# Offset bound on ScalarE, a third tap on TensorE, one product for the roots, and key rows stored in two parts

## The chip, the cores and the metric

The program runs on one core of one Trainium2 chip. A core has five instruction streams that run side by side and meet only through semaphores: TensorE (PE in the profile, with its weight loads as PEld), VectorE (DVE), ScalarE (ACT), GpSimd (POOL) and SyncE (SP), which here only starts DMA transfers. Sixteen DMA engines carry out the transfers. The metric is the device time of one execution in microseconds, from the first instruction to the last; lower is better.

## The reference, cut to what matters

The network has four layers over x of shape 8 x 56 x 56 x 128 in float32. Two of them are touched.

Layer 0 is a deformable convolution with a small MLP behind it. For each image:

```python
xp = x @ w_in + b_in
h = gelu(batch_norm(depthwise_conv_3x3(x) + dw_b))
offset = (h @ w_off + b_off)                       # 4 groups x 9 points x (x, y)
mask = softmax((h @ w_msk + b_msk), over the 9 points)
y = bilinear_samples(xp, at 3x3 grid + offset, weighted by mask) @ w_out + b_out
x = x + gamma1 * layer_norm(y)
x = x + gamma2 * layer_norm(gelu(x @ w_fc1 + b_fc1) @ w_fc2 + b_fc2)
```

Layer 1 whitens x. Layer 2 is self-attention with 8 heads of 16 channels, where queries, keys and values are one projection (`h = x @ W_k.T`), and then a mixture of experts. Layer 3 is linear attention and another mixture of experts. Of layers 1 and 3 and of the experts nothing is changed.

## The kernel before, in words

Within one layer's scope the instructions are put in order by a planner: the program text gives the data dependences and the priority (earlier text first), and the planner, which has its own idea of how long things take, lets a later instruction go ahead on an engine when an earlier one isn't ready. Buffers are rings of `bufs` tiles; a ring's next tile waits until the one that it replaces is released by all its readers. Attention itself (`attend`) is ordered by hand. A run-time `If` stands at the end of each of three stages, and nothing moves across it.

**Stage A, `conv_layer`, lines 128 to 398: the first half of layer 0.** The constants are loaded, and a tile of zeros (L236) is stored by ScalarE's DMA queue into the two edge rows at the top and bottom of `strips` (L239 to L242) and into the edge columns (L243 to L247). Then the images go through a software pipeline (L377 to L389). `image` loads one image, transposes it (L266), copies it into a padded picture (L271) and stores a copy `xT` (L276 to L279). `first_taps` makes the first `NTE` = 2 of the nine depthwise taps on TensorE, as products with a diagonal matrix per tap (L315), seven blocks of 448 columns, and ScalarE copies each block to `acc` (L322). `other_taps` adds the other seven on VectorE, one instruction for each tap over the whole picture of 128 x 3136 (L327). `projection` makes `xp` for two images at a time (L288, L295) and stores it (L301 to L305). `hidden` is the gelu on ScalarE (L341). `offsets` makes offsets and mask scores (L356, L363), takes the largest offset and the largest negative offset over 112 x 2016 numbers with two VectorE reductions (L365, L366) into two columns of `far`, does the softmax (L430 to L435, its exponential on ScalarE at L432) and stores the result (L370). At the end the maximum of `far` over all (L393 to L397) is compared with 1.0 (L398): only if no offset is beyond one pixel is the fast way of sampling taken, and the inputs at hand do take it.

**Stage B, `sample_near`, `norm` and `mlp`, lines 447 to 655.** Sampling is done as products with 88-row windows; the weights of the next image are built (L490 to L513) and transposed (L523, L525) while the current image is in flight. Each image has 7 groups of 448 columns, and each group passes through `norm` twice, 112 times in all. `norm` (L593 to L622) works on channels by pixels: squares on ScalarE (L600), sums of squares as products with a column of 1/128 (L604), which come out as `rs`, 112 pixels x 4, then + eps (L608) and the power -0.5 on GpSimd (L609). The roots have to be spread over the 128 channels for the product at L621. That is done by four products (L614): the weights are a column of `rs` repeated 128 times, the moving side is the 112 x 112 identity.

**Stage C** is layer 1.

**Stage D, `attention_keys`, lines 1039 to 1133.** For each of the 8 images: two loads (L1062), a store of the same tokens (L1063), layer norm (L1067, L1068, L1141, L112), transposes (L121, L122), then the keys `kT`: for each of two groups of four heads a tile of 128 rows, head j in rows 32j to 32j+15, a row of ones in 32j+16, and zeros in 32j+17 to 32j+31 (they come out of padded weights and a bias, L1083 to L1092). The tile has one buffer (`bufs=1`). Each group is stored whole to `kT_d` by SP, 128 rows of 12,544 bytes (L1094). Then the values (L1098 to L1108) are stored (L1110), and a bound is taken (L1117 to L1120). All transfers of this stage are on SP's queue. Behind the stage comes an `If`, and then `attend` loads keys and values part by part (L1222, L1224).

**Stage E** is `attend`, and **stage F** the rest.

Of the kernel before, what the change touches and what calls it, by code (L numbers as in the profile page):

```python
# [17 lines left out]
NB, IH, IW, C = 8, 56, 56, 128  # L18
S = IH * IW
T = 112  # L20
# [15 lines left out]
R4 = 4 * C  # L36

NPX = 6
NTE = 2


WB, WCOLS, WSTEP, WITER, WEPS = 64, NB * S * C // 64, 9, 5, 0.01
# [20 lines left out]
def make_consts(tc, pool):  # L63
    nc = tc.nc
    k = Consts()
    k.ident = pool.tile([128, 128], F32, name="ident")
    make_identity(nc, k.ident)
    k.eps = pool.tile([128, 1], F32, name="eps_col")
    nc.vector.memset(k.eps, EPS)
    k.mhalf = pool.tile([128, 32], F32, name="mhalf")  # L70
    nc.vector.memset(k.mhalf, -0.5)
    k.part = pool.tile([128, 1], F32, name="part_of_c")
    nc.vector.memset(k.part, 1.0 / C)
    k.ones = pool.tile([1, 128], F32, name="ones_row")
# [50 lines left out]

def conv_layer(tc, k, x, w, z):

    nc = tc.nc  # L130
    n_batch = x.shape[0]
    with ExitStack() as ctx:
# [63 lines left out]
        gam = row_bc(nc, cp, w["gamma2"], T, "gam2r")  # L196
        nc.vector.tensor_tensor(q.sft2, q.sft2, gam, ALU.mult)

        far = cp.tile([T, 2 * n_batch], F32, name="far")
        near = cp.tile([1, 1], I32, name="near")  # L200
        with ExitStack() as pre:
            ip = pre.enter_context(tc.tile_pool(name="l0i", bufs=1))
# [11 lines left out]
                "b_om",  # L214
            )
            b_om = b_om.unsqueeze(1).to_broadcast([T, GT, 3 * GP])

            dw = ip.tile([C, 9], F32, name="dw")
            nc.sync.dma_start(dw, w["dw_w"].rearrange("c a b d -> c (a b d)"))
# [13 lines left out]
            nc.vector.tensor_tensor(bn_t, bn_t, bn_s, ALU.mult)  # L233
            nc.vector.tensor_tensor(bn_t, bn_t, bn_b, ALU.add)

            zero = ip.tile([NX * n_batch, 2 * SW * C], F32, name="zero")  # L236
            nc.gpsimd.memset(zero, 0.0)
            rows = q.strips.rearrange("n k y s c -> (n k) y (s c)")
            for y in (0, VW - 2):  # L239
                nc.scalar.dma_start(  # L240
                    rows[:, y : y + 2].rearrange("k y s -> k (y s)"), zero
                )  # L242
            for n in range(n_batch):  # L243
                for at in (q.strips[n, 0, :, :2], q.strips[n, NX - 1, :, SW - 2 :]):
                    nc.scalar.dma_start(
# [104 lines left out]
            def offsets(n, hT):  # L350

                om = hp.tile([T, NT, 3 * GP], F32, name="om")
                for r in range(PH):
                    p = ps.tile([T, GT, 3 * GP], F32, tag="m", name="p_om")
                    for i in range(GT):
                        nc.tensor.matmul(  # L356
                            p[:, i, :],
                            hT[:, r, i].rearrange("p a b -> p (a b)"),
                            w_om,
                            start=True,  # L360
                            stop=True,
                        )
                    nc.vector.tensor_tensor(om[:, r * GT : (r + 1) * GT, :], p, b_om, ALU.add)  # L363
                off = om[:, :, : 2 * GP]
                nc.vector.tensor_reduce(far[:, 2 * n : 2 * n + 1], off, AX.XY, ALU.max)  # L365
                nc.vector.tensor_reduce(  # L366
                    far[:, 2 * n + 1 : 2 * n + 2], off, AX.XY, ALU.min, negate=True
                )
                mask_softmax(nc, hp, om)
                nc.sync.dma_start(q.om[n], om)  # L370


# [4 lines left out]
            for n in range(-1, n_batch + 1):  # L377
# [10 lines left out]
                if n > 0:  # L388
                    offsets(n - 1, hT)  # L389


            top = ip.tile([T, 1], F32, name="far_top")
            nc.vector.tensor_reduce(top, far, AX.X, ALU.max)  # L393
# [1 line left out]
            nc.tensor.transpose(p, top, k.ident[:T, :T])  # L395
            one = ip.tile([1, 1], F32, name="far_one")
            nc.vector.tensor_reduce(one, p, AX.X, ALU.max)  # L397
            nc.vector.tensor_scalar(near, one, 1.0, None, ALU.is_le)  # L398

        taken = nc.values_load(near[0:1, 0:1], min_val=0, max_val=1)  # L400
        with tc.If(taken > 0) as both:
# [191 lines left out]
def norm(tc, k, wp, ps, p, bias):  # L593


    nc = tc.nc
    y = wp.tile([C, QC], F32, name="y")
    nc.scalar.activation(y, p[:, :QC], AF.Identity, bias=bias)
    sq = wp.tile([C, QC], F32, name="sq")
    nc.scalar.activation(sq, p[:, :QC], AF.Square, bias=bias)  # L600
    yield
    var = p[:T, QC : QC + GT]
    for i in range(GT):
        nc.tensor.matmul(  # L604
            var[:, i : i + 1], sq[:, i * T : (i + 1) * T], k.part, start=True, stop=True
        )
    rs = wp.tile([T, GT], F32, name="rs")
    nc.vector.tensor_scalar(rs, var, EPS, None, ALU.add)  # L608
    nc.gpsimd.tensor_tensor(rs, rs, k.mhalf[:T, :GT], ALU.pow)  # L609
    yield  # L610

    p = ps.tile([C, QC], F32, tag="m", name="p_rs")
    for i in range(GT):
        nc.tensor.matmul(  # L614
            p[:, i * T : (i + 1) * T],
            rs[:, i : i + 1].to_broadcast([T, C]),
            k.ident[:T, :T],
            start=True,
            stop=True,
        )  # L620
    nc.vector.tensor_tensor(y, y, p, ALU.mult)  # L621
    return y  # L622

# [415 lines left out]
def attention_keys(tc, k, w, yv, tok, kT_out, va_out, low, small):  # L1039
# [6 lines left out]
    with ExitStack() as ctx:  # L1046
# [12 lines left out]
        for n in range(n_b):  # L1059
            t_sb = bp.tile([T, NT, C], F32, name="t")  # L1060
            for h in range(2):
                nc.sync.dma_start(t_sb[h * IW : (h + 1) * IW], yv[h, n])  # L1062
            nc.sync.dma_start(tok[n].rearrange("(t p) c -> p t c", p=T), t_sb)  # L1063
            mv = bp.tile([T, NT, 2], F32, name="mv")
            st = bp.tile([T, NT, 6], F32, name="st")
            for i in range(NT):
                nc.vector.bn_stats(st[:, i], t_sb[:, i])  # L1067
                nc.vector.bn_aggr(mv[:, i], st[:, i])  # L1068
            rs = rsqrt(nc, k, bp, mv, NT)
            xT = bp.tile([C, S], F32, name="xT")  # L1070
            for g in range(NG):
                xn = bp.tile([T, GT, C], F32, name="xn")
                for i in range(GT):
                    normalize(nc, xn[:, i], t_sb[:, g * GT + i], mv, rs, g * GT + i)
                transpose_group(
                    nc, k, ps, "m", xT[:, g * QC : (g + 1) * QC], xn, nc.scalar.copy
                )
            kT = bp.tile([128, 2, S], F32, name="kT", bufs=1)
            for g in range(2):
                for c in range(NG):  # L1080
                    cols = slice(c * QC, (c + 1) * QC)
                    p = ps.tile([128, QC], F32, tag="m", name="p_h")
                    nc.tensor.matmul(  # L1083
                        p, wk[:, g * 128 : (g + 1) * 128], xT[:, cols], start=True, stop=True
                    )
                    if c % 2:
                        nc.scalar.activation(
                            kT[:, g, cols], p, AF.Identity, bias=w.one16, scale=DK**-0.25
                        )
                    else:  # L1090
                        nc.vector.tensor_scalar(
                            kT[:, g, cols], p, DK**-0.25, w.one16, ALU.mult, ALU.add  # L1092
                        )
                nc.sync.dma_start(kT_out[n, g], kT[:, g])  # L1094
            va = vas[n % 2]
            for t, m in key_tiles():
                p = ps.tile([128, 2, 4, DK], F32, tag="m", name="p_v")
                nc.tensor.matmul(  # L1098
                    p[:m].rearrange("p g j d -> p (g j d)"),
                    xT[:, t * 128 : t * 128 + m],  # L1100
                    w.wv,
                    start=True,
                    stop=True,
                )
                if t % 2:
                    nc.scalar.copy(va[:m, :, t, :, :DK], p[:m])
                else:
                    nc.vector.tensor_copy(va[:m, :, t, :, :DK], p[:m])  # L1108
            for g in range(2):
                nc.sync.dma_start(va_out[n, g], va[:, g].rearrange("p t j d -> p (t j d)"))  # L1110

            sq = bp.tile([128, 2 * KT * 4, DK], F32, name="sq", bufs=1)
            v = va.rearrange("p g t j d -> p (g t j) d")[:, :, :DK]
            nc.gpsimd.tensor_tensor(sq, v, v, ALU.mult)  # L1117
            top = bp.tile([128, 2 * KT * 4], F32, name="top")
            nc.vector.tensor_reduce(top, sq, AX.X, ALU.add)
            nc.vector.tensor_reduce(tops[:, n : n + 1], top, AX.X, ALU.max)  # L1120
# [1056 lines left out]
    return t, b  # L2177


def token_layers(tc, k, a, y, out):  # L2180

    nc = tc.nc
    n_b = out.shape[0]
    with ExitStack() as ctx:
# [3 lines left out]
        t_c = [dp.tile([S, C], F32, name=f"t_c{n}") for n in range(n_b)]  # L2188
        t_g = dp.tile([n_b, S, C], F32, name="t_g")
        tok = [dp.tile([S, C], F32, name=f"tok{n}") for n in range(n_b)]  # L2190
        kT_d = dp.tile([n_b, 2, 128, S], F32, name="kT_d")
# [99 lines left out]
def conv_attn_hybrid_kernel(ctx, tc, a, out):  # L2291
# [7 lines left out]
    conv_layer(tc, k, a["x"], w, z)  # L2299
    whiten_layer(tc, k, z, y)  # L2300
    token_layers(tc, k, a, y, out.rearrange("n h w c -> n (h w) c"))


# [40 lines left out]
```

## Time and profile before

| what | value |
|---|---|
| time, median of 3 runs | 7714.85 us (7708.21 to 7727.53) |
| the profiled execution's own time | 7718.14 us |
| its span, first to last instruction | 7716.3 us |
| PE busy | 6482.3 us, 84% of the span |
| DVE busy | 5284.8 us, 68% |
| ACT busy | 4142.6 us, 54% |
| POOL busy | 2935.1 us, 38% |
| DMA queue of SP (q1) | 1260.76 MB, 65.1% of 16 engines' time |
| HBM read and written | 286.04 MB and 197.81 MB |

The stages stand one behind the other, so a mean over the span tells little; a table of busy time by stage is the first thing to look at. Lines of the profile name the source line (L327), the engine, the operation, the tiles, the shapes and the count, then the busy time, the mean of one in ns, and the idle time before them with what ended it. In the view by stretches, each engine's busy us and count are followed by the granted TensorE clock (1.00 is full), the mean busy share of the 16 DMA engines and the GB/s that they moved. The profile's packet records give start, length and size of each piece that a DMA engine moved; they say when, but not on which of the sixteen.

### The profile page before, as it was taken

To read this page: it belongs to the slowest core of one execution; us is meant where nothing else is said; L and a number is where in the kernel's file an instruction comes from. 1 tells how busy PE (TensorE), PEld (TensorE's weight loads), DVE (VectorE), ACT (ScalarE), POOL (GpSimd) and SP (SyncE) were. 2 spreads that over 40 slices of the span, in tenths; PEclk is the share of its full clock that TensorE was granted. 3 is DMA by queue.
4 is the path that set the end of the run, shared out by engine and by line. 5 is a ranking of instruction groups with operands and counts; after the bars stand their busy time and mean duration, and the time that the engine had idled before them with its cause. 6 is when DMAs were issued, how large, how long until landed. Compare 5 with 4: busy or idle time off the path is not lost. (4 is left out here: it accounts for less than half of the span.)

```text
span 7716.3 us, 157926 instructions
## 1 busy us (share of the span) xinstructions
PE 6482.3 (84%) x59883; PEld 2880.7 (37%) x59883; DVE 5284.8 (68%) x9856; ACT 4142.6 (54%) x6467; POOL 2935.1 (38%) x2555
## 2 busy tenths in 40 slices
PE   6659999556899999999999999999999997556654
PEld 4446666334233323323323323333333333245532
DVE  7975564366677777777777777777777776366752
ACT  4424444122666666666666666666666664056740
POOL 0011111022444444444444444444444443434653
PEclk8768898777999999999999999999999998788766
DMA  5453443376788778778778778778778775543543
GB/s 155 137 119 76 86 95 65 82 240 207 199 203 197 193 192 199 189 192 201 191 184 204 188 183 207 183 191 205 185 190 206 182 190 137 196 117 107 134 135 130
DMA packets 736303, 1287.38 MB, mean 167 GB/s; under 512 B 117698, under 2 KB 503108, under 8 KB 728516
## 3 DMA queue, kind: packets, MB, share of 16 engines
q1 hardware_dynamic: 725556, 1260.76, 65.1%
q0 software_dynamic: 6144, 12.60, 0.6%
q8 instruction: 484, 7.93, 0.5%
q10 hardware_dynamic: 3824, 3.68, 0.2%
q14 instruction: 295, 2.42, 0.1%
HBM read 286.04 MB, written 197.81 MB: 63 GB/s over the span
## 5 line engine op out<-in xcount | busy, mean ns | idle before, releaser
L1260 ACT ACTIVATE e<-p_s 128x768 f32<-128x768 f32 (+2 forms) x3712 | 2887.8, 830 | 1584.9 <-PE p_s L1252 1329.8
L1298 POOL COPY x<-sq 32x1152 f32<-32x1152 f32 x1792 | 2059.2, 1149 | 2067.6 <-PE p_s L1252 1330.0
L1271 DVE STREAM_TRANSPOSE sq<-e 128x768 f32<-128x768 f32 x2688 | 2434.5, 950 | 567.3 <-ACT e L1260 312.9
L1252 PE MATMUL p_s<-q,kT 32*128 32x384 f32 (+2 forms) x14848 | 1888.6, 548 | 33.6 <-ACT e L1260 18.6
L1305 PE MATMUL av<-e,va 128*32 128x384 f32 (+2 forms) x14848 | 1645.3, 515 | 30.4 <-DVE acc L1324 20.7
L1305 PE MATMUL avx<-x,va 128*32 128x384 f32 x10752 | 1138.3, 496 | 69.5 <-issue 40.2
L1252 PEld LDWEIGHTS p_s<-q,kT 32*128 32x128 f32 (+1 forms) x14848 | 654.8, 181 | 1252.6 <-issue 825.4
L1305 PEld LDWEIGHTS av<-e,va 128*32 128x32 f32 (+1 forms) x14848 | 294.5, 108 | 1049.4 <-issue 941.7
L1305 PEld LDWEIGHTS avx<-x,va 128*32 128x32 f32 x10752 | 353.2, 111 | 650.9 <-issue 595.2
L609 POOL TENSOR_TENSOR rs<-rs,mhalf 112x4 f32<-112x4 f32 x112 | 116.1, 1036 | 788.3 <-DVE rs L608 788.3
L1324 DVE TENSOR_TENSOR acc<-acc,avx 128x384 f32<-128x384 f32 x336 | 183.9, 547 | 229.9 <-PE avx L1305 228.6
L121 PE MATMUL p_tr<-ident,xn 112*128 112x112 f32 x672 | 134.6, 341 | 187.4 <-DVE xn L112 141.8
L1141 POOL TENSOR_TENSOR rs<-rs,mhalf 112x4 f32<-112x4 f32 (+2 forms) x136 | 168.1, 1236 | 269.3 <-DVE ntop L1942 123.8
L525 ACT COPY wT<-p_w 88x448 f32<-88x448 f32 x152 | 138.0, 922 | 194.1 <-PE p_w L523 161.4
L1990 ACT ACTIVATE xn<-t,ms,rs 112x128 f32<-112x128 f32 x448 | 185.3, 488 | 76.4 <-DVE ms L1983 76.4
L327 DVE SCALAR_TENSOR_TENSOR acc<-xp,dw,acc 128x3136 f32<-128x3136 f32 x56 | 194.3, 3478 | 31.3 <-ACT acc L322 31.2
L637 PE MATMUL p_f<-x1T,w 128*128 128x448 f32 x448 | 205.6, 583 | 4.4 <-DVE x1T L632 2.7
L121 PEld LDWEIGHTS p_tr<-ident,xn 112*128 112x128 f32 x672 | 98.7, 169 | 285.0 <-issue 185.1
L1385 POOL TENSOR_TENSOR rs<-rs,mhalf 128x3 f32<-128x3 f32 (+1 forms) x72 | 58.5, 815 | 365.0 <-DVE rs L1384 343.0
L523 PE MATMUL p_w<-ident,wide 112*88 112x112 f32 x896 | 146.5, 303 | 58.6 <-DMA px<-strips 34.1
L621 DVE TENSOR_TENSOR y<-y,p_rs 128x448 f32<-128x448 f32 x112 | 69.3, 619 | 176.6 <-PE p_rs L614 176.6
L122 ACT COPY xT<-p_tr 128x448 f32<-128x448 f32 x112 | 59.6, 532 | 229.8 <-PE p_tr L121 203.7
(354 smaller groups left out, 7830.9 us busy)
## 6 DMA issues: line engine op xcount, KB each, us to landing
x<-sq SPq DMA_DIRECT2D x5376, 144.0 KB
w<-in_L_ffn_weight_dram SPq DMA_DIRECT2D x64, 1024.0 KB
px<-strips SPq DMA_DIRECT2D x64, 616.0 KB
va_d<-va SPq DMA_DIRECT2D x16, 1600.0 KB
xT_d<-xT SPq DMA_DIRECT2D x112, 224.0 KB
xT<-xT_d SPq DMA_DIRECT2D x112, 224.0 KB
kT_d<-kT SPq DMA_DIRECT2D x16, 1568.0 KB
t<-t_a SPq DMA_DIRECT2D x16, 1568.0 KB
```

The costliest lines, as they stand in the source:

```text
L121: nc.tensor.transpose(p[:, i, :], src[:, i, :], k.ident[:T, :T])
L327: nc.vector.scalar_tensor_tensor(acc, xp[:, j // 3 : j // 3 + IH, j % 3 : j % 3 + IW], dw[:, j : j + 1], acc, ALU.mult, ALU.add,)
L523: nc.tensor.transpose(p[:, g], around[:, :, g], k.ident[:T, :T])
L637: nc.tensor.matmul(p, q.w1[:, f * 128 : (f + 1) * 128], x1T, start=True, stop=True)
L1141: nc.gpsimd.tensor_tensor(rs, rs, k.mhalf[:m, :n], ALU.pow)
L1252: nc.tensor.matmul(ss[j // 2][:m, j % 2, :width], kT[rows, 128 * i : 128 * i + m], q[rows, :width], start=True, stop=True,)
L1260: nc.scalar.activation(e[:m, 2 * j : 2 * j + 2, :width], ss[j][:m, :, :width], AF.Exp)
L1271: nc.vector.transpose(sq[:, :, i, j : j + 2].rearrange("p s j c -> p j s c"), exps[u, b, a, i][:, j : j + 2, :QB].rearrange("p j (s c) -> ...
L1298: nc.gpsimd.tensor_copy(*moves.pop(0))
L1305: nc.tensor.matmul(out, keys[u, b][1][:m, i, j, :], e[j], start=start, stop=stop)
L1324: nc.vector.tensor_tensor(to, to, in_order(av), ALU.add)
L1990: nc.scalar.activation(out[:, i], x[:, i], AF.Identity, bias=ms[:, i : i + 1], scale=rs[:, i : i + 1])
```

## The change

Five edits, in the order of the text:

1. `NTE` goes from 2 to 3: a third tap is made on TensorE, and VectorE makes six instead of seven.
2. The bound on the offsets moves. Instead of two reductions on VectorE ahead of the softmax, ScalarE makes four activations behind it: relu(+off - 1) and relu(-off - 1), each over half of the 28 x 72 offsets of a pixel row, with the sum kept by `accum_out`. `far` has four columns for each image, and the test is now "not above 0.0".
3. The tile of zeros is half as wide, so the edge rows of `strips` take four stores instead of two.
4. `norm` makes a diagonal matrix `own` on VectorE, 112 x 4 x 112 (identity times `rs`), and spreads the roots with one product, whose weights are a constant of ones.
5. `kT_d` is made before layer 0. In each of 8 rounds of stage A, SP stores the zero rows of one image's keys: 8 stores of 15 rows, each row in four pieces of 784 numbers out of the tile of zeros. In stage D each group's keys are then stored without those rows: four stores of 17 rows in place of one of 128.

The diff, cut to its core:

```diff
-NTE = 2
+NTE = 3
...
+    k.all = pool.tile([128, C], F32, name="all_ones")
+    nc.vector.memset(k.all, 1.0)
...
-            zero = ip.tile([NX * n_batch, 2 * SW * C], F32, name="zero")
+            zero = ip.tile([NX * n_batch, SW * C], F32, name="zero")
...
-            for y in (0, VW - 2):
-                nc.scalar.dma_start(
-                    rows[:, y : y + 2].rearrange("k y s -> k (y s)"), zero
-                )
+            for y in (0, 1, VW - 2, VW - 1):
+                nc.scalar.dma_start(rows[:, y], zero)
...
-                nc.vector.tensor_reduce(far[:, 2 * n : 2 * n + 1], off, AX.XY, ALU.max)
-                nc.vector.tensor_reduce(
-                    far[:, 2 * n + 1 : 2 * n + 2], off, AX.XY, ALU.min, negate=True
-                )
                 mask_softmax(nc, hp, om)
+                over = ip.tile([T, NT // 2, 2 * GP], F32, name="over")
+                for a in range(4):
+                    nc.scalar.activation(
+                        over,
+                        off[:, a // 2 * NT // 2 : (a // 2 + 1) * NT // 2],
+                        AF.Relu,
+                        bias=minus,
+                        scale=1.0 - 2.0 * (a % 2),
+                        accum_out=far[:, 4 * n + a : 4 * n + a + 1],
+                    )
                 nc.sync.dma_start(q.om[n], om)
...
                 if n > 0:
                     offsets(n - 1, hT)
+                    for g in range(2):
+                        for j in range(4):
+                            rows = kT_d[n - 1, g, 32 * j + DK + 1 : 32 * j + 32]
+                            nc.sync.dma_start(
+                                rows.rearrange("p (a s) -> p a s", a=4),
+                                zero[16 * j : 16 * j + 31 - DK, : S // 4]
+                                .unsqueeze(1)
+                                .to_broadcast([31 - DK, 4, S // 4]),
+                            )
...
-            nc.vector.tensor_scalar(near, one, 1.0, None, ALU.is_le)
+            nc.vector.tensor_scalar(near, one, 0.0, None, ALU.is_le)
...
+    own = wp.tile([T, GT, T], F32, name="own")
+    nc.vector.tensor_tensor(
+        own,
+        k.ident[:T, :T].unsqueeze(1).to_broadcast([T, GT, T]),
+        rs.unsqueeze(2).to_broadcast([T, GT, T]),
+        ALU.mult,
+    )
     yield
-
     p = ps.tile([C, QC], F32, tag="m", name="p_rs")
-    for i in range(GT):
-        nc.tensor.matmul(
-            p[:, i * T : (i + 1) * T],
-            rs[:, i : i + 1].to_broadcast([T, C]),
-            k.ident[:T, :T],
-            start=True,
-            stop=True,
-        )
+    nc.tensor.matmul(
+        p, k.all[:T], own.rearrange("p i t -> p (i t)"), start=True, stop=True
+    )
     nc.vector.tensor_tensor(y, y, p, ALU.mult)
...
-                nc.sync.dma_start(kT_out[n, g], kT[:, g])
+                for j in range(4):
+                    rows = slice(32 * j, 32 * j + DK + 1)
+                    nc.sync.dma_start(kT_out[n, g, rows], kT[rows, g])
```

The rest of the diff hands `kT_d` from the top function to `conv_layer` and `token_layers`.

More of the change, by code (lines that the diff above doesn't have):

```diff
@@ L122, in transpose_group, with conv_layer @@
     copy(dst, p.rearrange("p a b -> p (a b)"))
-def conv_layer(tc, k, x, w, z):
+def conv_layer(tc, k, x, w, z, kT_d):
     nc = tc.nc
@@ L197, in conv_layer @@
         nc.vector.tensor_tensor(q.sft2, q.sft2, gam, ALU.mult)
-        far = cp.tile([T, 2 * n_batch], F32, name="far")
+        far = cp.tile([T, 4 * n_batch], F32, name="far")
         near = cp.tile([1, 1], I32, name="near")
@@ L216, in conv_layer @@
             b_om = b_om.unsqueeze(1).to_broadcast([T, GT, 3 * GP])
+            minus = ip.tile([T, 1], F32, name="minus")
+            nc.vector.memset(minus, -1.0)
             dw = ip.tile([C, 9], F32, name="dw")
@@ L2177, in gate_weights, with token_layers @@
     return t, b
-def token_layers(tc, k, a, y, out):
+def token_layers(tc, k, a, y, kT_d, out):
     nc = tc.nc
@@ L2190, in token_layers @@
         tok = [dp.tile([S, C], F32, name=f"tok{n}") for n in range(n_b)]
-        kT_d = dp.tile([n_b, 2, 128, S], F32, name="kT_d")
         va_d = dp.tile([n_b, 2, 128, KT * 128], F32, name="va_d")
@@ L2298, in conv_attn_hybrid_kernel @@
     w = {n.removeprefix("L0_conv_"): v for n, v in a.items() if n.startswith("L0_")}
-    conv_layer(tc, k, a["x"], w, z)
+    kT_d = dp.tile([n_b, 2, 128, S], F32, name="kT_d")
+    conv_layer(tc, k, a["x"], w, z, kT_d)
     whiten_layer(tc, k, z, y)
-    token_layers(tc, k, a, y, out.rearrange("n h w c -> n (h w) c"))
+    token_layers(tc, k, a, y, kT_d, out.rearrange("n h w c -> n (h w) c"))
 _L0 = [
```

## The prediction

> **What bounds the kernel now.** I read the table by stretches first, then, within each touched stage, the costliest groups, the waits, the order of time and the packet records.
>
> ```profile
> 0.00:430.00 430.00, 264.52 (x1345) 206.82 (x1345) 368.86 (x255) 187.22 (x248) 13.68 (x9) 0.81 0.54 149
> 430.00:1430.00 1000.00, 865.85 (x11088) 612.66 (x11088) 571.41 (x1395) 433.10 (x657) 144.49 (x121) 0.86 0.37 80
> 1590.00:1949.00 359.00, 202.52 (x864) 134.45 (x864) 236.78 (x887) 85.70 (x200) 83.05 (x17) 0.70 0.68 217
> 1949.00:6480.00 4531.00, 4361.78 (x41481) 1433.42 (x41485) 3405.14 (x4894) 2918.83 (x3814) 2141.62 (x1890) 0.98 0.80 193
> ```
>
> Columns: PE, PEld, DVE, ACT, POOL, clock, DMA share, GB/s. Stage A (430 us) is VectorE's: 368.9 us busy, and from 55 us on 358.2 of 380. Stage B is TensorE's: 865.9 of 1000. In stage D (1590 to 1949) no engine is full. Attention is untouched.
>
> ```profile
> L327 DVE SCALAR_TENSOR_TENSOR acc<-xp,dw,acc 128x3136 f32<-128x3136 f32 x56 | 194.3, 3478 | 31.3 <-ACT acc L322 31.2
> L365 DVE TENSOR_REDUCE far<-om 112x1 f32<-112x2016 f32 x8 | 18.0, 2255 | 0.0
> L366 DVE TENSOR_REDUCE far<-om 112x1 f32<-112x2016 f32 x8 | 18.0, 2246 | 0.0
> L614 PE MATMUL p_rs<-ident,rs 112*128 112x112 f32 x896 | 130.0, 292 | 9.6 <-POOL rs L609 9.6
> L1742 DVE TENSOR_TENSOR own<-ident,choices 128x512 f32<-128x512 f32 x16 | 13.7, 862 | 1.8 <-issue 1.8
> DVE st L1067 <- DMA t<-y: 13.6, 2, 7.9
> ACT va L1106 <- DMA kT_d<-kT: 0.6, 1, 0.6
> kT_d<-kT SPq DMA_DIRECT2D x16, 1568.0 KB
> ```
>
> The last three are stage D's: all stores of keys together kept an engine waiting 0.6 us, loads of tokens 13.6 us. Stage D is a chain through PE, DVE and POOL, about 42 us an image (key stores issued at 1628.8 and, for the eighth image, 1922.5: 293.7 / 7). Its DMA work is hidden.
>
> **Stage A, term by term.** Removed from VectorE: 8 taps and 16 reductions. Instructions overlap a little; from start to next start a tap takes 3.39 us and a reduction 2.16 us (127.65 to 131.04, 131.04 to 133.20). 8 x 3.39 + 16 x 2.16 = 27.1 + 34.6 = **61.7 us**.
>
> Added to TensorE: 56 blocks x 2 passes (28 products of 128x448 took 10.73 us, 0.38 each) = 43 us. PE goes from 246 us to 289 of the 318 us that are left behind 55 us: covered, except for the first picture. VectorE waited 29.8 us for its blocks; a block now takes 6 passes for 4, seven blocks 14 x 0.38 = 5.4 us more, some of it at half clock: 6 us lost. If the cover went, PE would set the pace: per pair of images it has about 71 us at full clock against VectorE's 92.3 - 2 x 3.39 - 4 x 2.16 = 77.
>
> Added to ScalarE: 32 activations of 112x1008. The nearest row, the exponential L432, takes 1.04 us; rows with an accumulator show 0.19 to 0.21 us for reading it. 32 x 1.25 = 40 us on an engine busy 175 of 380; 5 us an image behind the exponential, in a queue that often waits for VectorE (76 us at L341). Taken at nothing; if all of it showed, 40 us.
>
> Added to SP and the DMA engines: 64 zero stores, 12.0 MB. Issue about 0.4 us each (edge columns, 60 rows: 0.42), 26 us of a queue that waits over 250 us. Moving them, at the packet rate of 26.5 GB/s an engine and 15 engines, 30 us. They need only the tile of zeros, so the planner may place them before the first `xT` stores; ScalarE has two `xT` buffers (23.2 us of waiting there now) and would be held. Cost 0 to 30 us; I take 6, nearer the low end because the share here is 0.51. The two extra edge stores (0.35 us) fall where ScalarE waits 7.0 us for a load. The last image's four activations run beside its softmax on VectorE (18.6 us from the last L363 to the last L435), so the branch isn't later for them. Stage A: 61.7 - 6 - 6 = **-50 us**, between -62 and -15.
>
> **Stage B.** Four products with their weights, in two passes each, are replaced by one of 448 columns:
>
> ```profile
> 801.98 1.06 PE L614 MATMUL p_rs<-ident,rs 112*128 112x112 f32 x8
> 802.88 3.19 PE L642 MATMUL p_f<-hid,w 128*128 128x448 f32 x8
> ...
> 806.78 0.93 PE L558 MATMUL p_y<-smp,w_out 128*128 128x448 f32 x2
> 807.54 0.93 PE L523 MATMUL p_w<-ident,wide 112*88 112x112 f32 x8
> ```
>
> Starts give 0.90 us for the eight, 0.76 us for one product of 448 columns. 112 x 0.14 = 16 us, up to 25 where the clock is half. VectorE gets 112 x `own`; L1742 scaled to 448 columns is 0.75 us, 84 us in an engine 57% busy: covered. But the chain from the power to the product grows by it, about 0.9 us with the semaphores, plus what VectorE has queued behind an `own` that waits for the power (1.0 us): copies of wT, whose wait PE feels. In time order p_rs starts a median 2.45 us after its power, so most have room; 10 of 112 start within 0.1 us of it, 9 us at 0.9 each; I take 8. Stage B: -16 + 8 = **-8 us**, from -25 to +15.
>
> **Stage D: here the change turns over.** Bytes fall: 64 stores x 17 rows for 16 x 128, 1088 rows for 2048. But what counts is over how many DMA engines a store is spread, and the rows show that this hangs on its row count. Stores of 128 rows: 15.8 packets in flight in the packet records, share 1.05 (neighbours overlap a little). Stores of `strips` (56 rows), with several queued: 12.9 in flight, share 0.82.
>
> ```profile
> 1631.00:1638.00 7.00, 7.00 (x51) 5.89 (x50) 6.82 (x38) 3.84 (x12) 0.00 (x0) 1.00 1.05 422
> 219.00:234.00 15.00, 15.00 (x76) 9.73 (x75) 14.82 (x8) 9.32 (x17) 0.00 (x0) 1.00 0.82 222
> ```
>
> 14 is the largest number up to 16 that divides 56. The load of b_inr, **113 rows** (divided by none), ran as 113 packets of 512 B strictly one after another, 2.65 us for what a 128-row load of the same packets did in 0.38 us. I read: a transfer uses as many engines as the largest divisor of its rows up to 16, and a prime count above 16 gets one. 17 is such a count; the zero stores' 15 rows get 15.
>
> A 12,544 B row takes 0.473 us on its engine (26.5 GB/s), so a store takes 17 x 0.473 = 8.0 us on one engine: eight to an image, 64.3 us against the 42 us that an image has. With queued `strips` stores the engines stay at 14 and don't fill the other two, so I take it that each transfer starts at the same engine and all 64 meet on one: 64 x 8.04 = 515 us. The same engine carries its sixteenth of the values (67 us) and of the token loads and stores behind 1638 (87 us), in order of issue. From the first key store, 1628.9 + 515 + 67 + 87 = 2298 us; only then do attention's loads, at 1948.7 now, pass. **+349 us**, and about 1 us an image of gaps where SP waits for a load before it issues: **+355**. `kT` has one buffer, so the next keys wait for these stores: a wait of some 50 us an image on DMA.
> Low end: everything else beside the 515: 1629 + 515 - 1949 = +195. High end: 12 us of gaps an image (its 7 us of key work plus issue): +445.
>
> The Trainium skill, "DMA: Bandwidth & Descriptors", section "Why a DMA increments its semaphore by 16 and not by 1", speaks against this edit: a queue of SP uses the largest k up to 16 that divides both sides' slowest dimension, always the lowest-numbered k engines, with 127 partitions as an example of one. The rows show the count; that one-engine stores share their engine is shown here only through the 56-row stores. The page's Specifications give about 27 GiB/s an engine; by that a store would take an estimated 7.4 us and the 64 stores 471 us, 44 us less, but 0.473 us a row is measured.
>
> **Sum.** 7718.1 (the profiled execution's own time) - 50 - 8 + 355 = 8015. That execution lay 3.3 us above the median: **8012 us**. Low: 7714.9 - 62 - 25 + 195 = 7823. High: 7714.9 - 15 + 15 + 445 = 8160.
>
> **Rivals.**
> - *The stores spread, and it is faster.* One mechanism: the one-engine stores go to different engines, or 17 rows are cut finer. The busiest engine then carries 64.3 / m + 19 us an image; the stage keeps its 42 us from m = 3 on, and the sum is 7714.9 - 58 = 7657 (7630 to 7715). For it: no row shows two one-engine transfers at once. Against it: the 113-row load wasn't cut, and the 56-row stores didn't rotate. 0.13.
> - *The zeros hold up stage A as well.* All 64 are issued ahead of the first `xT` stores, 30 us of transfers stand before them, ScalarE and then VectorE wait: 24 us more, 8036. For it: nothing in the data holds them back. Against it: the loads of the first images are earlier in the text. 0.07, on top of the forecast.
> - *The offsets' test answers otherwise* and the general path is taken: the sum of relu(|offset| - 1) is zero exactly when no offset exceeds 1, so nothing.
>
> **How the numbers follow.** Forecast 0.79, rivals 0.13 and 0.07, 0.01 for the rest. The range 7823 to 8160 holds the forecast and the second rival. Faster by over 0.3% (23 us, about what a measurement of this kernel tells from no change): 0.12; within: 0.02; slower: 0.86.
>
> **What would show it.** Right: stage D takes about 715 us with a DMA share under 0.5 though it waits for DMA, ScalarE and VectorE waiting at `kT` for kT_d stores; stage A ends near 385 us with no L365 and 48 taps; p_rs is 224 instructions. Wrong: key stores moving several at a time and stage D near 360 us (first rival); `xT` activations waiting over 40 us (second); POOL or DVE waits ahead of p_rs over 20 us (stage B's term).

## The result, and the profile after

The changed kernel takes 8201.91 us (median of 4, 8198.54 to 8209.75) where the kernel before takes 7711.53 us (median of 4): **1.0638 times as long, 95% interval 1.0625 to 1.065**. The forecast was 8012 us, the range 7823 to 8160: slower, as forecast, but by 490 us instead of 300.

Where the time went is read by stage. A stage ends here where SP issues the first load of the next one (the loads of `om`, of `x` from `z`, of `t`, and attention's of `kT`); this puts the end of stage A before at 441.0 us.

| us | A | B | C | D | the rest | span |
|---|---|---|---|---|---|---|
| before | 441.0 | 995.4 | 153.1 | 359.2 | 5767.6 | 7716.3 |
| after | 544.0 | 989.8 | 153.6 | 745.5 | 5764.1 | 8197.0 |
| difference | **+103.0** | -5.6 | +0.5 | **+386.4** | -3.5 | +480.7 |
| forecast | -50 | -8 | 0 | +355 | 0 | +297 |

The view by stretches of the changed kernel; columns as in the one of before (busy us and count of PE, PEld, DVE, ACT, POOL, then clock, DMA share, GB/s):

```profile
1743.00:1750.00 7.00, 2.37 (x9) 1.55 (x9) 5.57 (x13) 0.53 (x1) 4.09 (x1) 0.50 0.06 27
0.00:544.00 544.00, 299.66 (x1457) 232.56 (x1457) 312.21 (x236) 225.10 (x312) 12.82 (x9) 0.80 0.57 142
544.00:1527.00 983.00, 848.74 (x10416) 539.63 (x10416) 628.33 (x1504) 433.75 (x657) 143.47 (x121) 0.87 0.38 80
1687.00:2433.00 746.00, 214.05 (x866) 138.61 (x865) 242.96 (x887) 84.81 (x200) 83.04 (x17) 0.60 0.28 88
```

The first row is a stretch in which only key stores move: share 0.06, that is 1 of 16 engines, and 27 GB/s, where the 128-row stores of before showed 1.05 and 422 GB/s. Stage D (fourth row) doubles while every engine does what it did; its share falls from 0.68 to 0.28. Stage A (second row) is the surprise: VectorE is busy 312 us instead of 373, as meant, and the stage is still 103 us longer. Its waits, and behind the dots those of stage D (engine, line, what it waited for, us in total, times, longest):

```profile
PE p_x L269 <- DMA xs<-in_x_dram: 173.2, 5, 53.4
DVE acc L330 <- ACT acc L325: 169.0, 5, 38.8
DVE pj L298 <- PE p_in L291: 28.7, 32, 0.9
...
DVE st L1089 <- DMA t<-y: 192.6, 4, 62.7
ACT kT L1109 <- DMA kT_d<-kT: 154.1, 4, 39.2
DVE kT L1113 <- DMA kT_d<-kT: 122.3, 3, 41.7
```

In stage A, TensorE waits 173 us for the images; VectorE's 169 us at its first tap are the same waits two steps later. The kernel before has 31.2 us in place of the latter, and in place of the former:

```profile
PE p_x L266 <- DMA xs<-in_x_dram: 32.3, 1, 32.3
```

In stage D the key stores that kept an engine waiting 0.6 us before now keep ScalarE and VectorE waiting 276 us together, and the tokens keep VectorE waiting 193 us. The rows that answer to the groups shown of before:

```profile
L330 DVE SCALAR_TENSOR_TENSOR acc<-xp,dw,acc 128x3136 f32<-128x3136 f32 x48 | 166.9, 3480 | 169.3 <-ACT acc L325 169.0
L372 ACT ACTIVATE over<-om,minus 112x1008 f32<-112x1008 f32 x32 | 36.3, 1136 | 72.1 <-DVE om L366 71.5
L632 DVE TENSOR_TENSOR own<-ident,rs 112x448 f32<-112x448 f32 x112 | 70.0, 625 | 100.9 <-POOL rs L629 99.6
L640 PE MATMUL p_rs<-own,all_ones 112*128 112x448 f32 x224 | 117.2, 607 | 8.2 <-DVE own L632 8.1
```

**Why the images come late** is read from the order of time of SP's list (start, us, line, transfer, count) and of TensorE's transposes of the images:

```profile
180.22 0.34 SPq L380 DMA_DIRECT2D om_d<-om  x1
180.65 0.38 SPq L282 DMA_DIRECT2D xT_d<-xT  x1
181.08 8.87 SPq L404 DMA_DIRECT2D kT_d<-zero  x6
190.06 0.73 SPq L263 DMA_DIRECT2D xs<-in_x_dram  x1
...
413.19 0.35 SPq L380 DMA_DIRECT2D om_d<-om  x1
413.59 5.31 SPq L404 DMA_DIRECT2D kT_d<-zero  x3
419.00 0.86 SPq L263 DMA_DIRECT2D xs<-in_x_dram  x1
```

```profile
201.23 4.78 PE L269 MATMUL p_x<-ident,xs 112*128 112x112 f32 x28 [53.40 <-DMA xs<-in_x_dram]
288.13 5.46 PE L269 MATMUL p_x<-ident,xs 112*128 112x112 f32 x28 [38.30 <-DMA xs<-in_x_dram]
325.76 5.46 PE L269 MATMUL p_x<-ident,xs 112*128 112x112 f32 x28 [10.63 <-DMA xs<-in_x_dram]
429.93 4.78 PE L269 MATMUL p_x<-ident,xs 112*128 112x112 f32 x28 [39.88 <-DMA xs<-in_x_dram]
```

The planner has put the zero stores into SP's list between the `xT` stores, and the image loads behind them: each of the last four loads now stands behind two more `om` stores than before (2, 3, 3 and 5 of them instead of 0, 1, 1 and 3). SP works its list off in order, so a load waits for all that stands ahead of it: for the `om` store of an earlier image, which comes at the end of VectorE's chain, and for the zeros, whose 64 issues hold SP for 102 us, mostly 1 to 2 us each. A load needs only the buffer of the image two before it. TensorE is done with these at 80.0, 126.5, 206.0 and 293.6 us, and the loads are issued 109 to 150 us after that (before: 2 to 30 us). TensorE starts 10.9 to 11.9 us after each load's issue: the loads aren't slow, they are issued late. The issue times of the last four loads, with the two experiments below that bear on them:

| us | image 5 | 6 | 7 | 8 |
|---|---|---|---|---|
| before | 73.2 | 159.6 | 175.5 | 251.9 |
| after | 190.1 | 276.3 | 314.7 | 419.0 |
| loads issued by GpSimd (`xs_pool`) | 82.2 | 137.1 | 166.9 | 222.5 |
| zeros issued by GpSimd (`z_pool`) | 125.5 | 200.1 | 215.6 | 287.7 |

### The profile page after: what moved, and what is told of

Same layout as the page of the kernel before. It is cut to its first block, busy times and chain, and to the rows that moved or that the text cites. A ratio compares the mean times of both kernels' runs of the same rounds, so it can differ in the third digit from the quotient of the medians.

```text
span 8197.0 us, 157122 instructions
## 1 busy us (share of the span) xinstructions
PE 6503.4 (79%) x59323; PEld 2829.6 (35%) x59323; DVE 5287.3 (65%) x9947; ACT 4180.9 (51%) x6531; POOL 2934.1 (36%) x2555
## 5 line engine op out<-in xcount | busy, mean ns | idle before, releaser
L330 DVE SCALAR_TENSOR_TENSOR acc<-xp,dw,acc 128x3136 f32<-128x3136 f32 x48 | 166.9, 3480 | 169.3 <-ACT acc L325 169.0
L1105 PE MATMUL p_h<-xT,wk 128*128 128x448 f32 x224 | 107.8, 637 | 142.0 <-ACT kT L1109 142.0
```

The source lines that it names most:

```text
L330: nc.vector.scalar_tensor_tensor(acc, xp[:, j // 3 : j // 3 + IH, j % 3 : j % 3 + IW], dw[:, j : j + 1], acc, ALU.mult, ALU.add,)
```

## The experiments

Two theories for stage A: the zeros' **place** in SP's list, or their **transfers** (3840 pieces of 3136 B, 0.298 us each); a third, that edits 1 and 2 lengthen the chain. For stage D: **one engine** for every store of 17 rows, against the number of stores or the single buffer. Stages by the same rule as above, from one profiled run each; what no edit touches ("the rest") lies between 5757 and 5790 us in these runs, so single runs' totals are compared to some 15 us, their stages more closely. The experiments ran in three sets, beside which the kernel before took 7727.8 us (the first four rows), 7715.8 (the next four) and 7723.7 (the last four); across sets, ratios to it compare better than medians. "In flight" is the number of packets that move at the same moment.

| us | A | B | D | median |
|---|---|---|---|---|
| `e_1to4` edits 1 to 4 | 399.7 | 992.1 | 360.3 | 7691.4 |
| `e_whole_D` keys stored whole | 543.7 | 1003.6 | 360.0 | 7840.0 |
| `k16` 16 rows a store | 569.8 | 996.6 | 377.0 | 7872.8 |
| `z_pool` zeros by GpSimd | 446.1 | 985.7 | 747.3 | 8115.7 |
| `xs_pool` image loads by GpSimd | 501.3 | 990.6 | 744.5 | 8146.5 |
| `two_q` key stores on two queues | 543.3 | 989.3 | 718.5 | 8165.3 |
| `s_far` edits 2 and 3 | 414.6 | 997.9 | 360.3 | 7687.7 |
| `s_nte` edit 1 | 415.8 | 997.8 | 359.4 | 7686.7 |
| `k17_b2` two buffers for kT | 543.1 | 992.8 | 747.7 | 8218.9 |
| `p4` rows in four pieces | 546.5 | 989.1 | 745.0 | 8210.8 |
| `z_late` zeros in stage B, 16 rows | 399.4 | 1080.6 | 381.6 | 7789.4 |
| `e_1to3` edits 1 to 3 | 395.8 | 997.7 | 359.9 | 7682.7 |

**e_1to4: all but the fifth edit.** The loop of zero stores is taken out, and:

```diff
-                for j in range(4):
-                    rows = slice(32 * j, 32 * j + DK + 1)
-                    nc.sync.dma_start(kT_out[n, g, rows], kT[rows, g])
+                nc.sync.dma_start(kT_out[n, g], kT[:, g])
```

> The change without its fifth edit: no zeros stored in stage A, each group's keys stored whole (128 rows) as before. In the changed kernel stage A takes 544 us instead of 441 and stage D 746 instead of 359. Theory 1 (the 64 zero stores are what costs stage A its time, by their places in SP's list or by their transfers; edits 1 and 2 are worth what was predicted): stage A ends near 390 us, stage B gives 6 us, stage D is 359 us as before, in all about 7718 - 50 - 6 = 7662 us. Theory 2 (the third tap on TensorE or ScalarE's four activations lengthen the chain of stage A): stage A stays above 500 us, in all 7800 us or more.

0.9949 of the kernel before (0.9932 to 0.9965), stage A 399.7 us. The third theory falls: all of stage A's loss, 544.0 - 399.7 = 144 us, is the zeros'. The gain, 41 us, is less than the 56 expected; why is settled below.

**e_whole_D: the zeros stay, stage D stores whole again.** The same diff, with the zero loop left in.

> The changed kernel with one thing undone: stage D stores each group's keys whole again, 128 rows in one store; the zeros are still stored in stage A. Theory 1 (the stores of 17 rows all run on one DMA engine, and that alone is stage D's loss): stage D returns to about 359 us, with some 16 key packets in flight, stage A stays at 544, in all about 8199 - 387 = 7812 us. Rival (stage D is late because stage A leaves something behind, or because kT_d is now made before layer 0): stage D stays near 746 us, 8199 us in all.

Stage D 360.0 us, and 16 key rows in flight by the median of the packet records (13 in the mean). The 17-row stores alone are stage D's loss. The total is 28 us above the 7812 expected, from parts that this edit leaves alone: stage B took 14 us more in this run than in the changed kernel, the rest 16.

**k16: as many stores, but of 16 rows.** `zero[96:97]` is set to one after the edge stores; early rows come from `zero[96:112]`.

```diff
-                            rows = kT_d[n - 1, g, 32 * j + DK + 1 : 32 * j + 32]
+                            rows = kT_d[n - 1, g, 32 * j + DK : 32 * j + 32]
...
-                    rows = slice(32 * j, 32 * j + DK + 1)
+                    rows = slice(32 * j, 32 * j + DK)
```

> The row of ones goes with the zeros: 16 rows a head are stored early (one of ones, 15 of zeros) and stage D stores 16 rows a head instead of 17, still in eight stores an image; 64 rows more in stage A and 64 fewer in stage D. Theory 1 (the row count decides: 17 has no divisor up to 16 but one, 16 has sixteen): a store's rows go to 16 engines, stage D falls from 746 to 360 to 375 us, in all about 7815 us. Rival (eight stores instead of two are the price: their issue, their completions, or the narrow slices of 16 partitions): stage D stays above 650 us, above 8100 us in all. Stage A stays near 544 us under both.

One row less a store, and stage D falls from 746 to 377 us:

```profile
1717.00:2094.00 377.00, 202.15 (x866) 133.97 (x865) 243.49 (x887) 85.68 (x200) 83.05 (x17) 0.70 0.71 173
```

The DMA share (next to last) is 0.71 again; its packet records show 16 key rows in flight by the median (13 in the mean) where 17-row stores show 1.0. The row count decides, not the number of stores. But it is 17 us worse than whole stores (360), though it moves half the bytes: a row now took 1.39 us in the mean, where it took 0.48 in whole stores, so the 1024 rows took 1423 us of the DMA engines' time together, against 991 for the 2048 of `e_whole_D`. The loads of tokens, for which VectorE waited 13.2 us there, pay for it:

```profile
DVE st L1090 <- DMA t<-y: 32.5, 4, 9.1
```

The rows of such a store lie in 16 neighbouring partitions; whether that is what slows them was not tested. Stage A rose by 26 us, which was not expected; with it, the zeros' pieces, now all read from the same 16 partitions, took 0.41 us instead of 0.298.

**z_pool: the zeros on GpSimd's queue.** `nc.sync` becomes `nc.gpsimd` in the zero loop.

> The changed kernel with the zero stores of stage A issued by GpSimd instead of SP: the same 3840 pieces of 3136 B, but none in SP's list, where the loads of the images are again three ahead and then one round earlier. Stage D keeps its stores of 17 rows. Theory 1a (place: standing in SP's list, the zeros push the loads of the images behind stores that wait, so TensorE waits for the image): stage A ends near 390 us, in all about 8199 - 154 = 8045 us. Theory 1b (transfers: 3840 pieces x 0.298 us / 16 engines = 72 us of all the engines, in which image loads and xT stores stand): stage A stays above 500 us, in all 8155 us or more.

Between the two: stage A 446 us. 98 of the 144 us went when the zeros left SP's list. Up to some 19 of the 98 may be transfers, because GpSimd's queue moved the same bytes in another form: 1920 packets of 6272 B that took 838 us together, instead of 1142 us (the difference, over 16 engines, is 19). The other 46 are a new wait at the start: GpSimd, with nothing else to do, issued all 64 between 23 and about 100 us. ScalarE's own 16 edge stores of `strips` then took 42 us to issue instead of 19, so its first copies came 23 us later, and its `xT` copies waited 23 us for the stores of `xT` instead of 6 (up to 110 us). VectorE's wait for its first blocks grew from 36.6 (in `e_1to4`) to 79.8 us. The first of these lines is `e_1to4`'s, the others are `z_pool`'s:

```profile
22.30 19.02 ACTq L248 DMA_DIRECT2D strips<-zero  x16
22.28 42.33 ACTq L248 DMA_DIRECT2D strips<-zero  x16
DVE acc L330 <- ACT acc L325: 79.8, 2, 79.2
```

**xs_pool: the image loads off SP's list instead.** `nc.sync` becomes `nc.gpsimd` at L262.

> The changed kernel with the loads of the eight images issued by GpSimd instead of SP; the 64 zero stores stay in SP's list, stage D keeps its stores of 17 rows. With the zeros on GpSimd's queue stage A took 446 us, with none 400, in the changed kernel 544. Theory 1a (place: an image load that stands in SP's list behind an om store and behind zero stores is what stage A waits for): the loads go as soon as their buffer is free, TensorE's 173 us of waiting for images fall below 60, stage A ends between 400 and 450 us, in all about 8199 - 120 = 8080 us. Theory 1b (transfers: the image loads are slow because zeros move at the same time, or zeros hold the other stores of SP): stage A stays above 500 us, above 8155 us in all.

The last four loads go at 82 to 222 us (table above), each within 0.5 us of its buffer's coming free. TensorE's wait for images falls from 173 to 14 us, and VectorE's last instruction ends at 438.6 us instead of 522.0. But the stage ends at 501: what SP's list still holds by then, stores of `strips`, two `om` stores and 16 zeros, takes to 501 with the compute engines idle. So the bound of 450 was missed: that zeros hold SP's other stores was part of theory 1b, but at the end of the stage neither had looked for it.

```profile
437.00:501.00 64.00, 0.00 (x0) 0.00 (x0) 1.64 (x1) 0.00 (x0) 0.00 (x0) 0.50 0.82 199
```
```profile
466.75 2.57 SPq L380 DMA_DIRECT2D om_d<-om  x1
469.38 16.42 SPq L404 DMA_DIRECT2D kT_d<-zero  x8
485.91 0.80 SPq L380 DMA_DIRECT2D om_d<-om  x1
486.77 12.07 SPq L404 DMA_DIRECT2D kT_d<-zero  x8
```

So the late images were the place's first price, 83 us at VectorE's end; with them gone, the same 64 stores, mostly 1 to 2 us each in a list that must also carry the stage's last results, are its second: the stage itself ends only 43 us earlier.

**two_q: every second 17-row store on ScalarE's queue.**

```diff
-                    nc.sync.dma_start(kT_out[n, g, rows], kT[rows, g])
+                    (nc.scalar if j % 2 else nc.sync).dma_start(kT_out[n, g, rows], kT[rows, g])
```

> The changed kernel with every second of the eight stores of 17 rows issued by ScalarE's queue instead of SP's. If the one engine is given by the row count alone, both queues' stores meet on the same engine: still 1.0 key packets in flight and stage D near 746 us, 8199 us in all. If each queue has an engine of its own for such stores, two are in flight: the 515 us of packets are split into two halves of 258 beside some 150 of other traffic on SP's, stage D falls to 400 to 450 us, in all about 7870 us. Stage A stays at 544 us.

Still 1.0 key row in flight with both queues' rows in turn, stage D 718.5 us. The engine is the same for both queues. Of the 27 us saved, 15 are the rows' own time (524 us in all instead of 539); the rest was not traced. The stretch, in a part where little but keys moves:

```profile
1762.00:1768.00 6.00, 6.00 (x13) 3.14 (x13) 0.76 (x3) 1.06 (x2) 0.00 (x0) 0.54 0.07 30
```

**k17_b2: `kT` with `bufs=2`.**

> The changed kernel with two buffers for the keys' tile kT instead of one. In the changed kernel stage D takes 746 us and ScalarE and VectorE wait 276 us at kT for its stores. Theory 1 (the one DMA engine's throughput: 539 us of key rows, its sixteenth of 2048 values, 68 us, and its share of the tokens): the waits move to another place but stage D stays between 690 and 750 us, 8145 to 8200 us in all. Rival (one buffer: the wait between a store and the next keys, not the engine, sets the pace): stage D falls below 600 us, below 8055 us in all. Stage A stays at 544 us.

747.7 us, as the throughput theory has it (the total, 8218.9, lies above its 8200, since the rest took 18 us more in this run). The waits at `kT` are gone and stand at the tokens instead, which queue behind the keys on the same engine:

```profile
DVE st L1089 <- DMA t<-y: 309.4, 4, 100.8
```

**p4: each 17-row store written as 17 x 4 pieces of 784 numbers** (`rearrange("p (a s) -> p a s", a=4)` on both sides).

> The changed kernel with each store of 17 rows written as 17 x 4 pieces of 784 numbers, on both sides. If the number of pieces decides (68, whose largest divisor up to 16 is 4), four engines share a store, the busiest carries some 64 x 17 x 0.30 = 326 us, and stage D falls below 550 us, below 8005 us in all. If the number of partitions that the tile has, 17, decides, the store stays on one engine, in 68 pieces of 3136 B; these took 0.298 us each in stage A's zero stores, so 64 x 68 x 0.298 = 1297 us beside some 150 us of other traffic, and stage D rises to 1400 to 1500 us, 8850 to 8950 us in all. Stage A stays at 544 us under both.

745.0 us, and the packets are rows of 12,544 B as before: the four pieces, which lie one behind the other on both sides, were moved as one. Neither case came about; whether pieces or partitions decide is not told apart by it.

**s_far and s_nte: edits 2 and 3 alone, edit 1 alone.** The diffs are those parts of the change.

> The kernel before with edits 2 and 3 alone: the bound on the offsets by four activations of ScalarE behind the softmax, the zero tile half as wide. VectorE is spared 16 x 2.16 = 34.6 us. Edits 1 to 4 together brought stage A from 441 to 400 us, 41 us, where 56 were expected. Theory 1 (ScalarE's 40 us are covered, the 15 us are lost to edit 1): stage A ends near 441 - 34 = 407 us, in all 34 us below the kernel before. Rival (ScalarE's activations delay the gelu and the copies behind them): stage A ends at 415 to 425 us, 16 to 26 us below.

> The kernel before with edit 1 alone: the third tap on TensorE. VectorE is spared 8 x 3.39 = 27.1 us. Theory 1 (TensorE's 43 us are not covered where VectorE waits for it, the first picture's blocks and the projections: 5 us and 10 us): stage A ends near 441 - 10 = 431 us, in all 5 to 12 us below the kernel before. Rival (covered but for 6 us in the first picture, as predicted): stage A ends near 420 us, 21 us below.

`s_far` 0.9968 (0.9957 to 0.9979), stage A -26.4 us; `s_nte` 0.9965 (0.9953 to 0.9978), stage A -25.2. My theory that edit 1 was where the 15 us went is wrong: alone it gives what VectorE is spared but for 2 us. VectorE's end in each tells it apart. `s_far`: VectorE ends at 401.4 instead of 434.6, 33.2 us earlier (34.6 were expected), but the stage's end gains only 26.4. The stage ends when the last `om` store has landed. Before, the last two were issued 10 us apart and the last moved alone in 4.9 us; in `s_far` they come 5 us apart, while stores of `strips` still move, and the last is done 9.6 us after it starts. In both edits together:

```profile
0.00:400.00 400.00, 296.74 (x1457) 227.37 (x1457) 312.50 (x236) 221.81 (x312) 13.09 (x10) 0.91 0.60 164
```
```profile
DVE acc L330 <- ACT acc L325: 36.6, 1, 36.6
DVE pj L298 <- PE p_in L291: 24.5, 27, 0.9
```

VectorE is busy 60.9 us less, waits 5.4 more for its first blocks and 10.4 more for TensorE's projections (14.1 before), ends 47.0 us earlier, and 5.7 of these are lost behind the last stores: 41.3 us. TensorE's 43 us were covered but for some 2 us with edit 1 alone, where VectorE waits 16.6 us for the projections, and not quite with VectorE shortened by edit 2 as well.

**z_late: edit 5 with the zeros in stage B and 16 rows a store.** In `sample_near`, where `pad` is 16 x 392 numbers, a row of ones and 15 of zeros:

```diff
             for tick in range(2 * PH):
+                if tick < 8:
+                    rows = kT_d[n, tick // 4, 32 * (tick % 4) + DK : 32 * (tick % 4) + 32]
+                    nc.sync.dma_start(
+                        rows.rearrange("p (a s) -> p a s", a=8),
+                        pad.unsqueeze(1).to_broadcast([32 - DK, 8, S // 8]),
+                    )
```

> Edit 5 with both of its prices taken away: rows of ones and zeros (16 a head, one engine count of 16) are stored by SP in stage B instead of stage A, where the DMA share is 0.38, and stage D stores 16 rows a head. Edits 1 to 4 stay. (The general way of sampling, which the inputs do not take, would leave these rows unwritten.) Theory 1 (the zeros cost stage A its 144 us by their place there and nothing by themselves): stage A ends near 400 us as without zeros, stage B stays near 990 us, stage D takes 360 to 377 us, in all 7690 to 7710 us: no better than edits 1 to 4 alone, since stage D's stores were hidden before. Rival (zeros cost wherever they stand in SP's list): stage B is 40 us or more longer, 7735 us or more in all.

The rival: stage A 399.4, but stage B 1080.6 us, 88 more than in `e_1to4`; 1.0081 of the kernel before (1.0066 to 1.0096). TensorE now waits for the windows, which it did not before:

```profile
PE p_smp L557 <- DMA px<-strips: 44.9, 12, 10.7
```

That is half of the 88 us; VectorE's wait for `om` grows from 16 to 33 us, and the rest was not traced. Stage D, at 381.6 us, is above the 360 to 377 expected, with 16-row stores as slow as in `k16` (1.40 us a row). In both stages where they were tried, the zeros in SP's list made TensorE wait for its loads. (The general way of sampling, which the inputs don't take, would leave those rows unwritten.)

**e_1to3: without edit 4** (`own` and the one product).

> Edits 1 to 3 alone: as the kernel with edits 1 to 4, but the roots spread by four products of 112 columns instead of own and one product. Edits 1 to 4 gave 0.9949 of the kernel before, [0.9932, 0.9965]. As predicted (edit 4 is worth 8 us, between a gain of 25 and a loss of 15): 0.996. Rival (own and the wait for it take back what TensorE is spared): 0.995 or less. The stages' own spans tell more than the ratio: stage A ends near 400 us under both; stage B took 992 us with edit 4 and should take 1000 us without it under the first, 990 us or less under the second.

0.9946 (0.9932 to 0.996), against 0.9949 with edit 4: no difference that these runs can tell, so neither theory is settled by the ratio. Stage B is 997.7 us without and 992.1 with it. Over all profiles (without `z_late`) stage B's mean is 992.2 us in the nine kernels with edit 4 (985.7 to 1003.6) and 997.2 in the four without (995.4 to 997.9): some 5 us, of which no single run is proof. TensorE's busy time does fall, by 14 us (866.65 to 852.93).

`e_1to3` and `e_1to4` gain most on the kernel before, 0.5%; `s_far` and `s_nte` gain 0.3%.

## Why the prediction was right and wrong

- **Stage D, one engine for 17 rows: right, mis-sized by 31 us.** 386 us measured, 355 forecast. Of a row's 0.473 us the median is right (0.469), the mean is 0.495, because 135 rows that had packets of values beside them took 0.66 us in the mean, up to 1.59: 1088 rows took 538.8 us, not 515. With a sixteenth of the values' 1030 us (64, forecast 67) and of the 1341 us of tokens behind the first key store (84, forecast 87), the one engine is estimated to be busy 687 of the 707 us from the first key store to attention's loads; the remaining 20 us of gaps were forecast at about 6. The choice that all stores meet on one engine, which no row of before showed directly, is now shown, for two queues too. The packet records show it a second way: of each image's 256 rows of values, 240 move within 9 to 12 us, and then, 23 to 27 us later, the last 16, one sixteenth of them (before, all 256 within 8 to 11 us). The Trainium skill, "DMA: Bandwidth & Descriptors", section "Why a DMA increments its semaphore by 16 and not by 1", said the same of the row count, and that such transfers use the lowest-numbered engines; the runs agree that 17 rows get one, the same for all, and 16 rows sixteen (16 in flight by the median). Which number that engine has, no record here tells.
- **Stage A, the zeros: wrong, and this is the step that failed.** "Cost 0 to 30 us; I take 6": 144 us. Two things were wrong in it. The transfer time was taken at 26.5 GB/s an engine, the rate of 12,544 B rows in 128-row stores; the zeros' pieces of 3136 B took 0.298 us, 10.5 GB/s, so 3840 x 0.298 / 15 = 76 us on fifteen engines instead of 30. Their size alone does not explain it: the `xT` stores' pieces of 1792 B took 0.078 us (23 GB/s) in the same stage. What the zeros share with the rows of `k16` (9 GB/s) is a source of 15 or 16 neighbouring partitions, and the cause stays open. And the queue was priced by an issue of 0.4 us, 26 us for 64, and by the 250 us that it waits. An issue took 1.6 us in the mean, 102 us for 64, and SP's waiting isn't room: it waits at an instruction, and all that stands behind it waits too. The place in SP's list is worth an estimated 79 to 98 of the 144 us by `z_pool`. Most of that is the image loads pushed behind `om` stores: with the loads alone moved away, VectorE ends 83 us earlier. How the rest divides between slow transfers and place is not shown. The second rival had the sign, but not what happened: in the changed kernel the `xT` copies wait 6.7 us for their stores, where its sign was over 40. Zeros ahead of the first `xT` stores are what `z_pool` shows, at 46 us instead of 24.
- **Stage A, VectorE: right.** 61.7 us less forecast, 61.2 measured; first blocks 6 and 5.4. "If the cover went": it went in the projections, 10.4 us with both edits, 2.5 with edit 1 alone. "The branch isn't later for them": the branch wasn't, but the last `om` store was, 5.7 us. ScalarE's four activations an image (36.3 us in all) stayed covered: with them alone (`s_far`) VectorE ended 33.2 of 34.6 us earlier.
- **Stage B: right in sign as far as the runs tell.** -8 forecast, -5.6 in the profile, -5 between the means. 16 us less TensorE time forecast, 17.1 measured; `own` 0.625 us, 0.75 estimated. That TensorE time is real; the stage's end moves by about a third of it, which no single run proves.
- **The rivals.** That stores spread (0.13) is excluded by 1.0 packets in flight. The test takes the same branch, so that rival is nothing, as said.

The range ended 42 us too low: stage D's 31 us lie inside it, stage A's 153 (from -50 to +103) do not.

## What to carry to other kernels

Price an added DMA by its place in the issuing engine's list: find in the order of time which load would stand behind it and which late store stands ahead of both, and compare that load's issue time with the time its buffer comes free. Price a store by the number of engines that its row count lets it use before counting its bytes; here about half the bytes cost twice the stage, since 17 rows ran on one engine and 16 on sixteen. Then look at the time of one row: in stores of 16 rows it was three times that in stores of 128, so half the bytes took more time of the DMA engines, not less. And a store that is hidden behind other work brings nothing when it is made smaller: the whole stores kept an engine waiting 0.6 us, and no version with fewer bytes was faster in stage D.

## What the runs showed of the hardware

- Stores of 17 rows from two issuing queues (SP and ScalarE) shared one DMA engine: 1.0 row in flight throughout, 0.47 us each by the median. One sixteenth of the values' rows of an image (16 of 256) came 23 to 27 us after the others.
- Rows of 12,544 B that had packets of values beside them took 0.66 us in the mean, up to 1.59, the others 0.47.
- A row of 12,544 B took 1.39 us (9 GB/s) in stores of 16 rows on sixteen engines (`k16`), 0.48 us in stores of 128 rows. A 3136 B piece of a 15-row store took 0.298 us (10.5 GB/s), and 0.41 us when all pieces were read from the same 16 partitions; a 1792 B piece of a 128-row store took 0.078 us (23 GB/s).
- In the changed kernel, runs of five or more zero stores in SP's list took 1.1 to 2.4 us each to issue (5.63 us for 5, 14.52 for 6), a lone one mostly 0.92.
